# A convolution block in three stages: one instruction order across the seams, and what is loaded, stored and copied there

## The chip, the core and the metric

The kernel runs on one core of a Trainium2 chip. Its engines work side by side, each in its own order: TensorE (PE, matmuls; its weight loads are listed as PEld), VectorE (DVE), ScalarE (ACT), GpSimd (POOL) and SyncE (SP). SP and POOL start most transfers, and a transfer that must wait blocks what stands behind it on the engine that starts it. The metric is the device time of the whole program in microseconds, the median of several runs. A profile is one more execution, recorded by the hardware; its span runs from the first to the last instruction.

## The reference

The input x is 16 images of 192 channels and 64 by 64 pixels, float32. Cut to what matters:

```python
h = ln_over_channels(x)                                  # ln1
projected, gate = split(conv1x1(h, in_proj))             # 192 -> 384 channels
projected = depthwise3x3(projected, dw_k)
scanned = mix of four first-order recurrences of projected: along rows and columns, both ways
local = depthwise3x3(projected, le_k)
mixed = (scanned + local) * sigmoid(gate)
bn = (mixed - mean) / sqrt(var + 1e-5)                   # per channel, over all images and pixels
x = x + conv1x1(gelu(bn * bn_w + bn_b), out_proj)
h2 = ln_over_channels(x)                                 # ln2
x = x + conv1x1(gelu(conv1x1(h2, fc1)), fc2)             # 192 -> 768 -> 192
pooled = x.mean(over pixels)
w = a 3x3 kernel per image and channel, from a small net on pooled, four of its nine taps not zero
out = depthwise3x3(x, w) + bias
```

The batch norm needs the mean and the variance of a channel over all images, so nothing of the second half can start before the first half is done. This makes the seam between stages B and C.

## The kernel before

All is float32. Work falls into three stages, called A, B and C here.

**Stage A, projection.** 64 steps (`n` in the loop at L530), each eight image rows of two images, 512 pixels of each. `load_a` (L437) brings x, half on SP and half on POOL, three steps ahead. `turn` transposes pixels on PE for the variance, `project` (L471) multiplies by the input weights, and DVE and ACT evict the result into a staging buffer, scaled by the pixel's deviation (L485, L486). Four steps fill one block of 6.3 MB; 16 blocks alternate between two staging buffers, `stg0` and `stg1`. While a block is being filled, the one before is stored to HBM in four parts, one per step (`store`, L501): a part is a range of the 24 channel groups (`PARTS`, L47), and each part is a tensor of its own in HBM, `pg_d[0]` to `pg_d[3]`. Group 0 doesn't go to HBM: `store_first` (L495) copies it on chip into `low`. The first write of a block into its staging buffer waits for the stores of the block before last. After the last step its block is stored at once (L547 to L550). Beside the steps, small pieces of work (`beside`, from L394) prepare constants, among them `dv_d` and `lv_d`, from which stage B loads its banded matrices `dm` (depthwise) and `lm` (local and vertical), and load the weights of stage C (`load_weights`).

**Stage B, scans.** 96 steps (`k`, L711), each a pair of channels for all images; four pairs make a group. A step has `depthwise` of pair k+2 on PE, `tables` on ACT and two `scans` on DVE for pair k+1, `local` of pair k on PE, and for pair k-1 `vertical` on PE and `gate` on DVE, which multiplies with the sigmoid, writes the mixed rows over the group's own tile and takes the statistics (L666, L667). Three tiles hold groups in turn: part of `low`, `pg_o0` and `pg_o1`. `load_pg` (L567), on SP, loads group g+2 when group g-1 has been stored to `mixed_d` in HBM (L672, on POOL). Each group is 4 MB, each store 2 MB. `batch_norm` (L676) turns the statistics into a scale and a bias per channel, for the first 128 channels in the middle of the stage (L732) and for the other 64 at its end (L739): two matmuls, three DVE operations, more matmuls, the square root on ACT, and small DVE operations.

**Stage C, MLP and output.** Chunks of 512 pixels of an image pair. The mixed rows come back from `mixed_d` (`load_y`), DVE transposes them (`unmix`, L803, three 32 by 32 block transposes), ACT does batch norm and Gelu (L808, L809), `out_proj` multiplies (L819, L823) and DVE evicts into an image tile `ximg` (L826); `center`, `squares`, `normalize` are the second layer norm, `first` is fc1 (L884) with its Gelu (L887), `second` is fc2 (L774). The loop at L984 holds several chunks at different depths in one pass. Loads for the first chunks start at the end of stage B: `load_y` for `t` 0 and 1 at L735, and for `t` 2, which holds the last 64 channels, at L738, after the last group's store. The `ys` of chunks 2 to 7 lie in the second image tile until that is needed.

Each stage's instructions stand in a region of `manual_schedule` (L507, L704, L983), in which each engine keeps the written order. Buffers of a stage are released at its end, and a tile that takes their place waits for their last readers and writers. The transfers of a queue use eight semaphores in turn, so the ninth waits for the first.

Of the kernel before, what the change touches and what calls it, by code (L numbers as in the profile page):

```python
# [46 lines left out]
PARTS = ((1, 6), (6, 12), (12, 18), (18, NCG))  # L47
# [8 lines left out]
def conv_block_kernel(ctx: ExitStack, tc: tile.TileContext, x, prm, w_in, w_out, w_fc1, b_fc1, w_fc2, w1, bn1, w2, out):  # L56
# [7 lines left out]
    ORDER = {mybir.EngineType.PE, mybir.EngineType.DVE, mybir.EngineType.Activation, mybir.EngineType.SP,  # L64
             mybir.EngineType.Pool}

# [34 lines left out]
    wf2 = k2.tile([128, NFC, C], F32, tag="wf2", name="wf2")  # L101
# [71 lines left out]
    mats[0]["lm"] = lm_even  # L173
    bn_sc = cp.tile([128, 2], F32, tag="bn_sc", name="bn_sc")
# [9 lines left out]
    def load_lm(g):  # L184
        n = GC // 2
        for i, q in enumerate(HALF):
            v = lv_d[g, i, :, 0:1, :]
            src = bass.AP(v.tensor, v.offset, [[n, HW], [128 * n, 5], [1, HW * n]])
            (nc.sync, nc.gpsimd)[i].dma_start(mats[g % 2]["lm"][q].rearrange("p k m c -> p k (m c)"), src)
# [8 lines left out]
    def load_y(n, y, queues, ts=(0, 1, 2)):  # L198
# [4 lines left out]
        for t, q, i, c0 in ((0, slice(0, 128), 0, 0), (1, slice(0, 128), 1, 0), (2, HALF[0], 0, 128), (2, HALF[1], 1, 128)):  # L203
            if t in ts:
# [3 lines left out]
                for wh in range(2):  # L208
                    vw = v[32 * wh:32 * wh + 32].rearrange("w (q e) -> q w e", q=nq)
                    qd, k = (q, wh) if t < 2 else (HALF[wh], i)  # L210
                    if len(queues) == 1:
                        queues[0].dma_start(y[qd, t, k], vw)
                    else:
                        for b in range(nq):
                            p0 = qd.start + 32 * b
                            queues[b % 2].dma_start(y[p0:p0 + 32, t, k], vw[b])


    with ExitStack() as stage:
# [5 lines left out]
        w0 = wf2.rearrange("p m c -> p (m c)").rearrange("p (t n) -> p t n", t=3)  # L225
# [190 lines left out]
        for k in range(5):  # L416
            beside(40 + k, load_weights, k)
        beside(46, load_dm, 0)
        beside(47, load_lm, 0)
        beside(48, load_dm, 1)  # L420
        beside(50, lambda: finish_weights(0, bank()))
# [5 lines left out]
        stg = [stage.enter_context(tc.tile_pool(name=f"stg{i}", bufs=1)) for i in range(2)]  # L427
# [43 lines left out]
        def project(n):  # L471
            blk, part = divmod(n, per)
            if part == 0:
                both_i = stg[blk % 2].tile([128, 2, 2 * C, BR], F32, tag="stg", name="stg")
                stag[blk] = [both_i[:, i] for i in range(2)]
# [30 lines left out]

        with tc.manual_schedule(engines=ORDER):  # L507

            for dst, src in ((pt3, prm), (w0, w_in)):
                v = src.rearrange("(t p) n -> p t n", p=64)  # L510
                nc.sync.dma_start(dst[HALF[0]], v)
                nc.scalar.dma_start(dst[HALF[1]], v)
            make_identity(nc, ident)
            nc.vector.memset(mean_w, 1.0 / C)
            nc.vector.memset(ones, 1.0)
            nc.vector.memset(eps6, 1e-6)
            nc.vector.memset(eps5, 1e-5)
            nc.vector.memset(mask, 1.0)
            for k, r in ((0, 0), (1, HW - 1)):
                nc.vector.memset(mask[:, k, :, r:r + 1], 0.0)  # L520
            for c in range(3):
                load_a(c)
            centre = projection_weights()
            turn(0)
            for g in range(AR):
                variance(0, g)
            centre()
            deviation(0)

            for n in range(n_ac):  # L530
                if n + 3 < n_ac:
                    load_a(n + 3)
                blk, part = divmod(n, per)
                if blk:
                    if part == 0:
                        store_first(blk - 1)
                    store(blk - 1, part, (nc.gpsimd, nc.sync))
                    if part == per - 1:
                        stag.pop(blk - 1)
                if n + 1 < n_ac:  # L540
                    turn(n + 1)
                project(n)
                if n + 1 < n_ac:
                    deviation(n + 1)
                for f, args in side.pop(n, ()):
                    f(*args)
            store_first(blk)  # L547
            store(blk, 0, (nc.gpsimd, nc.sync))
            for d in range(1, len(PARTS)):
                store(blk, d, (nc.gpsimd, nc.gpsimd))  # L550


    with ExitStack() as stage:
        pg_odd = []
        kb = stage.enter_context(tc.tile_pool(name="kb", bufs=1))
        pg_odd.append(kb.tile([128, n_blk, 2, GC, BR], F32, tag="pg_o0", name="pg_o0"))
        wb = stage.enter_context(tc.tile_pool(name="wb", bufs=2))
        kc = stage.enter_context(tc.tile_pool(name="kc", bufs=1))
        late = {}
# [7 lines left out]
        def load_pg(g):  # L567
            s = grp[g]
            if g == 2:
                pg_odd.append(kc.tile([128, n_blk, 2, GC, BR], F32, tag="pg_o1", name="pg_o1"))  # L570
            s["pg"] = pg_even if g % 3 == 0 else pg_odd[g % 3 - 1]
            if g:
                d = [lo_ <= g < hi_ for lo_, hi_ in PARTS].index(True)
                lo_ = (g - PARTS[d][0]) * GE
                nc.sync.dma_start(s["pg"].rearrange("p n k c j -> p n (k c j)"),
                                  pg_d[d][:, :, :, lo_:lo_ + GE].rearrange("i b p e -> p (i b) e"))
# [51 lines left out]
        def lmul(k, m, src, dst, start, stop):  # L628
            g, c = divmod(k, hp_)
            for i, q in enumerate(HALF):  # L630
                for ih, o in enumerate(HALF):
                    nc.tensor.matmul(dst(bst[k]["ps"][i][o]), mats[g % 2]["lm"][q, m, :, c], src(q, ih), start=start, stop=stop)  # L632
# [25 lines left out]
        def gate(k):  # L658
# [10 lines left out]
            if c == hp_ - 1:  # L669

                for i0, i1 in ((0, n_half),) if g < NCG - 1 else ((0, 2), (2, n_half)):
                    nc.gpsimd.dma_start(mixed_d[i0:i1, :, :, g].rearrange("i b p e -> p (i b) e"),  # L672
                                        s["pg"][:, i0 * NB:i1 * NB, 0].rearrange("p n c j -> p n (c j)"))
                s.clear()

        def batch_norm(cls):  # L676

            chs = (slice(0, 128), slice(128, C))[cls]
            n = chs.stop - chs.start

            means = stats.rearrange("p c (e k) -> p k e c", k=3)[:, 1, :, chs]
            sums2 = stats.rearrange("p c (e k) -> p k e c", k=3)[:, 2, :, chs]
            dv = late["dev"][:, :, chs]
# [6 lines left out]
            nc.vector.scalar_tensor_tensor(dv, sums2, 2.0 / (n_half * HW), dv, ALU.mult, ALU.add)  # L690
            pq = psb.tile([128, CH], F32, tag="l", name="pq", bufs=4)
# [11 lines left out]

        with tc.manual_schedule(engines=ORDER):  # L704
            load_pg(0)
            load_pg(1)
            load_pg(2)
            mats[1]["lm"] = kc.tile([128, 5, HW, hp_], F32, tag="lm1", name="lm1")
            load_lm(1)
            late["dev"] = kc.tile([128, 2, C], F32, tag="dev", name="dev")  # L710
            for k in range(-2, n_bp + 1):  # L711
                if 0 <= k + 1 < n_bp:
                    tables(k + 1)
                if k >= 1:
                    vertical(k - 1)
                    gate(k - 1)
                    g, c = divmod(k, hp_)
                    if c == 0 and 0 < g < NCG - 1:
                        load_lm(g + 1)
                    if c == 0 and g + 2 < NCG:  # L720
                        load_pg(g + 2)
                    if c == hp_ - 2 and g + 2 < NCG:
                        load_dm(g + 2)
                if 0 <= k + 1 < n_bp:
                    scans(k + 1)
                if k + 2 < n_bp:
                    depthwise(k + 2)
                if 0 <= k < n_bp:
                    local(k)
                    sigmoid(k)  # L730
                if k == n_bp - 5 * hp_:
                    batch_norm(0)  # L732
                if k == n_bp - hp_:

                    load_y(0, y_low, (nc.sync,), (0, 1))  # L735
                    load_x2(0)
                    load_x2(1)
            load_y(0, y_low, (nc.sync, nc.gpsimd), (2,))  # L738
            batch_norm(1)  # L739
# [53 lines left out]
    def unmix(n):  # L793

        c, y = n % NCH, ys[n // 2]
        mx = mxs[n % 2]
        r0 = (c % 2) * CR
        for t in range(3):

            kinds = ("p k (c j) -> p j k c", "p (r k w) -> p r k w") if t < 2 else ("p k (c j) -> p k j c", "p (k r w) -> p k r w")  # L800
            blocks = y[:, t].rearrange(kinds[0], j=BR)
            blocks = blocks[:, r0:r0 + CR] if t < 2 else blocks[:, :, r0:r0 + CR]
            nc.vector.transpose(mx[:, t].rearrange(kinds[1], k=2, w=32), blocks)  # L803
        st[n].update(mx=mx)
# [168 lines left out]
    def at(f, n, *a):  # L973
        if 0 <= n < n_ch:
# [7 lines left out]

    with tc.manual_schedule(engines=ORDER):  # L983
        for n in range(-3, n_ch + 1):  # L984
            ended = (n - 1) // NCH if n >= NCH and (n - 1) % NCH == NCH - 1 else None
            if n + 5 < NCH and (n + 5) % 2 == 0:
                load_y(n + 5, ys[(n + 5) // 2], (nc.sync, nc.gpsimd) if n == -3 else (nc.gpsimd,))
# [84 lines left out]
```

## Time and profile before

| | |
|---|---|
| median of 3 runs | 3854.52 us (3853.04 to 3855.56) |
| the profiled execution | 3864.51 us, span 3862.7 us |
| stage A, 30 to 640 us | PE busy 595.2 of 610 us, DVE 457.0, ACT 239.8, DMA 241 GB/s |
| stage B, 720 to 1330 us | PE busy 602.8 of 610 us, DVE 600.3, ACT 514.1, DMA 272 GB/s |
| stage C, 1450 to 3800 us | PE busy 2349.8 of 2350 us, DVE 1442.5, ACT 906.1, DMA 58 GB/s |
| end of A, start of B, 640 to 720 us | PE busy 63.5 of 80 us, mean clock 0.89 |
| end of B, start of C, 1330 to 1450 us | PE busy 93.1 of 120 us, mean clock 0.87 |

A line of the timeline has the start and the length of a run of instructions, the engine, the source line, the operation, output and inputs, and in brackets how long the engine had been idle before and what ended that. `SPq` and `POOL ... DMA` lines are the starting of transfers, not the transfers. A line of the waits has the total, the number and the longest. A line of the windows has the stretch, then for PE, PEld, DVE, ACT and POOL the busy time and number of instructions, then PE's granted clock (1.00 is full), the mean busy share of the 16 DMA engines and the GB/s moved.

### The profile page before, as it was taken

What the parts mean: (1) busy time and instruction counts of PE and PEld (TensorE: products, weight loads), DVE (VectorE), ACT (ScalarE), POOL (GpSimd) and SP (SyncE); (2) the same over time, 40 slices, a digit from 0 to 9 for tenths busy, and PEclk for the clock granted to TensorE, in tenths of its full rate; (3) what the DMA queues carried; (4) which work ended last, traced back from release to release, by engine and by line L of the source; (5) the groups of instructions that cost most, each with busy time, mean ns of one, the idle gap of its engine ahead of it and who ended that gap; (6) DMA issues with size and microseconds to landing.
All of it is one profiled execution on the core that took longest, in us unless ns stands there. A gap on an engine that the chain in (4) does not pass through costs nothing.

```text
span 3862.7 us, 61441 instructions
## 1 busy us (share of the span) xinstructions
PE 3768.0 (98%) x25484; PEld 1750.0 (45%) x25484; DVE 2675.2 (69%) x4140; ACT 1775.7 (46%) x1879; POOL 411.3 (11%) x665
## 2 busy tenths in 40 slices
PE   8999999899999979999999999999999999999998
PEld 5565666566655533333333333333333333333333
DVE  6776776899999955456656756665765765674754
ACT  3333334788887833334334434333343433343442
POOL 2333332111101020000000000000000000000000
PEclk9999999999999989999999999999999999999999
DMA  6789987999999840112212222222222221221212
GB/s 152 234 235 237 269 263 245 270 274 283 274 284 258 230 99 21 53 43 60 74 55 63 66 65 59 69 58 64 70 55 59 70 69 44 76 72 44 69 28 71
DMA packets 305542, 491.13 MB, mean 127 GB/s; under 512 B 45344, under 2 KB 200208, under 8 KB 305264
## 3 DMA queue, kind: packets, MB, share of 16 engines
q1 hardware_dynamic: 246640, 290.58, 28.4%
q0 software_dynamic: 58208, 196.28, 19.0%
q8 instruction: 202, 3.31, 0.4%
q14 instruction: 76, 0.62, 0.1%
q10 hardware_dynamic: 416, 0.33, 0.0%
HBM read 284.98 MB, written 197.92 MB: 125 GB/s over the span
## 4 chain that ended last, share of the span: by engine, by line
PE 94%; DMA 3%; DVE 2%; issue 1%; ACT 0%; SPq 0%; POOL 0%; DVEq 0%; POOLq 0%; ACTq 0%
PE ps_f L884 27%; PE ps_f L774 25%; PE ps_pj L480 12%; PE ps_l L632 10%; PE ps_d L588 6%; PE ps_o L823 5%; PE ps_o L819 3%; PE ps_xt L455 2%; PE ps_v L846 1%; PE ps_m L846 1%; DMA pg_o<-pg_d 1%; DMA xa<-in_x_dram 1%; DMA out_dram<-ol 0%; PE ps_k L774 0%; DMA pg_d<-stg 0%
## 5 line engine op out<-in xcount | busy, mean ns | idle before, releaser
L884 PE MATMUL ps_f<-h,wf 64*128 64x512 f32 x4608 | 1050.7, 601 | 4.3 <-DVE h L874 3.6
L774 PE MATMUL ps_f<-gl,wf 128*64 128x512 f32 x4608 | 1021.5, 592 | 0.0
L887 ACT ACTIVATE gl<-ps_f,bf 128x1024 f32<-128x1024 f32 x384 | 428.2, 1115 | 1175.0 <-PE ps_f L884 1174.2
L884 PEld LDWEIGHTS ps_f<-h,wf 64*128 64x128 f32 x4608 | 433.7, 187 | 564.1 <-issue 561.9
L826 DVE SCALAR_TENSOR_TENSOR ximg<-ps_o,pt,low 128x256 f32<-128x256 f32 x384 | 168.3, 480 | 629.2 <-PE ps_o L823 629.1
L774 PEld LDWEIGHTS ps_f<-gl,wf 128*64 128x64 f32 x4608 | 330.5, 137 | 580.0 <-issue 537.9
L480 PE MATMUL ps_pj<-wi,xa 64*128 64x384 f32 x3072 | 518.5, 490 | 10.6 <-DVE stg L485 10.4
L486 ACT ACTIVATE stg<-ps_pj,rsa 128x384 f32<-128x384 f32 x256 | 239.5, 940 | 382.9 <-PE ps_pj L480 347.9
L480 PEld LDWEIGHTS ps_pj<-wi,xa 64*128 64x128 f32 x3072 | 293.1, 188 | 208.2 <-DVE stg L485 16.4
L68 DVE SCALAR_TENSOR_TENSOR o<-ximg,taps,o 128x1024 f32<-128x1024 f32 x252 | 323.7, 1285 | 86.0 <-ACT o L944 78.5
L948 POOL DMA_DIRECT2D out_dram<-o x168 | 87.9, 528 | 2134.3 <-DVE o L68 2131.5
L485 DVE TENSOR_SCALAR stg<-ps_pj,rsa 128x384 f32<-128x384 f32 x256 | 228.6, 893 | 109.6 <-PE ps_pj L480 84.7
L873 DVE RECIPROCAL rs<-rs 128x512 f32<-128x512 f32 x64 | 214.3, 3348 | 64.9 <-ACT rs L872 64.9
L623 DVE TENSOR_TENSOR_SCAN v<-tab,q 128x1024 f32<-128x1024 f32 x96 | 218.2, 2273 | 10.8 <-ACT tab L611 10.8
L625 DVE TENSOR_TENSOR_SCAN v<-tab,q 128x1024 f32<-128x1024 f32 x96 | 217.5, 2265 | 0.0
L823 PE MATMUL ps_o<-low,wo 128*64 128x256 f32 x1536 | 209.6, 394 | 0.0
L611 ACT ACTIVATE tab<-mask,dec_b 128x1024 f32<-128x1024 f32 x192 | 209.3, 1141 | 0.0
L588 PE MATMUL ps_d<-pg_o,dm 64*64 64x384 f32 (+2 forms) x2560 | 181.5, 424 | 13.1 <-DMA pg_o<-pg_d 13.1
L462 DVE BATCH_NORM_STATS2 st<-ps_xt 128x6 f32<-128x192 f32 x512 | 173.5, 339 | 23.8 <-PE ps_xt L455 23.8
L855 DVE TENSOR_TENSOR h<-ximg,ps_m 128x768 f32<-128x768 f32 x128 | 116.1, 948 | 98.7 <-PE ps_m L846 98.7
L588 PEld LDWEIGHTS ps_d<-pg_o,dm 64*64 64x64 f32 x2560 | 132.7, 198 | 91.3 <-issue 67.7
L803 DVE STREAM_TRANSPOSE low<-low 128x512 f32<-128x512 f32 x174 | 167.5, 1015 | 1.8
(182 smaller groups left out, 3771.7 us busy)
## 6 DMA issues: line engine op xcount, KB each, us to landing
pg_o<-pg_d SPq DMA_DIRECT2D x16, 4096.0 KB
low<-in_x_dram SPq DMA_DIRECT2D x128, 384.0 KB
out_dram<-o POOLq DMA_DIRECT2D x168, 256.0 KB, 3.7
pg_d<-stg POOLq DMA_DIRECT2D x102, 384.0 KB, 7.6
pg_d<-stg SPq DMA_DIRECT2D x90, 384.0 KB
mixed_d<-pg_o POOLq DMA_DIRECT2D x15, 2048.0 KB, 11.8
low<-mixed_d SPq DMA_DIRECT2D x116, 256.0 KB
low<-pg_d SPq DMA_DIRECT2D x7, 4096.0 KB
```

What stands on the lines that cost most here:

```text
L68: nc.vector.scalar_tensor_tensor(o, in0, scalar, in1, ALU.mult, ALU.add, **kw)
L480: nc.tensor.matmul(ps[i], pixels(n, t, g)[q], wi[q, t].rearrange("p g k c -> p (g k c)"), start=(t == 0), stop=(t == 2))
L485: nc.vector.tensor_scalar_mul(stag[blk][0][:, :, j], ps[0], rs[:, g, 0:1])
L486: nc.scalar.activation(stag[blk][1][:, :, j], ps[1], AF.Copy, scale=rs[:, g, 1:2])
L588: nc.tensor.matmul(dst(ps[o, ih]), mats[g % 2]["dm"][q, di + 1, :, ch], src(s["pg"][q, :, 0, ch]), start=(di == 0), stop=stop)
L623: nc.vector.tensor_tensor_scan(vf, tab, q, 0.0, ALU.mult, ALU.add)
L625: nc.vector.tensor_tensor_scan(vf[:, ::-1], tab[:, ::-1], q[:, ::-1], 0.0, ALU.mult, ALU.add)
L632: nc.tensor.matmul(dst(bst[k]["ps"][i][o]), mats[g % 2]["lm"][q, m, :, c], src(q, ih), start=start, stop=stop)
L774: nc.tensor.matmul(ps[q], w(i), rhs(i), start=start, stop=stop)
L823: nc.tensor.matmul(ps[q, wh].rearrange("p (r w) -> p r w", w=32), wo[:, 64 * t:64 * t + 64], cols(rows(s["mx"][:, i]))[:, :, wh], start=Fa ...
L884: nc.tensor.matmul(pf[:, i], wf1[q, t, 128 * m:128 * m + 128], s["h"][q, t], start=(t == 0), stop=(t == 2))
L887: nc.scalar.activation(gl, pf, AF.Gelu, bias=bf1[:, m:m + 1])
```

## The change

1. One region of `manual_schedule` is entered before stage A and holds to the end, instead of three.
2. `PARTS` is (1,2), (2,9), (9,16), (16,21), (21,24): the first part is group 1 alone. In the first step of a block two parts are stored, and then 7, 5 and 3 groups. After the last step only group 0 and the part of group 1 are stored at once (POOL); the other 16 stores follow on SP behind the load of group 1.
3. That load is split: images 0 to 5 of each half on SP, 6 and 7, which the last blocks write, on POOL.
4. The odd blocks' staging buffer `mid` lasts to the end of B: it is then the third group tile, `lm` of the odd groups and `dev`. So group 2's load waits for the last block's stores out of it.
5. `wf2` and `lm` of group 1 share a tile `place`: `lm` of group 1 is loaded in step 49 of A, and `wf2` in B at group 3 instead of in step 42 of A.
6. `batch_norm` is split: `spread` (matmuls and three DVE operations) and, one step later, the rest.
7. At the end of B the rows that chunks 0 and 1 need of the last group are copied on chip from its tile into `y_low` by four transfers, ahead of its store to HBM, which is one transfer instead of two; the other rows of `t` 2 are loaded half a group earlier. The transposes of chunk 0 stand between the steps of the second batch norm.
8. In C, chunk 2's transposes and Gelu move from before `out_proj` of chunk 1 to the end of that pass, and the memset of `pool2` moves three passes later.

```diff
-PARTS = ((1, 6), (6, 12), (12, 18), (18, NCG))
+PARTS = ((1, 2), (2, 9), (9, 16), (16, 21), (21, NCG))
...
-    wf2 = k2.tile([128, NFC, C], F32, tag="wf2", name="wf2")
+    place = k2.tile([128, 5 * HW * (GC // 2)], F32, tag="place", name="place")
+    wf2 = place[:, 0:NFC * C].rearrange("p (m c) -> p m c", m=NFC)
...
+    SB_ = 2 * 2 * C * BR
+    mid = ce.tile([128, SB_], F32, tag="mid", name="mid")
+    mats[1]["lm"] = mid[:, NPG:NPG + 5 * HW * (GC // 2)].rearrange("p (k m c) -> p k m c", k=5, m=HW)
+    dev = mid[:, NPG + 5 * HW * (GC // 2):NPG + 5 * HW * (GC // 2) + 2 * C].rearrange("p (e c) -> p e c", e=2)
+    lm_first = place.rearrange("p (k m c) -> p k m c", k=5, m=HW)
+    lm_of = lambda g: lm_first if g == 1 else mats[g % 2]["lm"]
...
+    LASTC = 32 - GC
+    def load_y(n, y, queues, ts=(0, 1, 2), last=32):
...
+                    if last < 32:
+                        for b, ncb in ((0, 32), (1, last)):
+                            p0 = qd.start + 32 * b
+                            queues[0].dma_start(y[p0:p0 + 32, t, k, 0:ncb * BR], vw[b, :, 0:ncb * BR])
...
+    def turn_back(y, mx, half, t):
+        kinds = ("p k (c j) -> p j k c", "p (r k w) -> p r k w") if t < 2 else ("p k (c j) -> p k j c", "p (k r w) -> p k r w")
+        blocks = y[:, t].rearrange(kinds[0], j=BR)
+        r = slice(half * CR, (half + 1) * CR)
+        nc.vector.transpose(mx[:, t].rearrange(kinds[1], k=2, w=32), blocks[:, r] if t < 2 else blocks[:, :, r])
+    ctx.enter_context(tc.manual_schedule(engines={
+        mybir.EngineType.PE, mybir.EngineType.DVE, mybir.EngineType.Activation, mybir.EngineType.SP, mybir.EngineType.Pool}))
...
-        for k in range(5):
+        for k in (0, 1, 3, 4):
             beside(40 + k, load_weights, k)
...
+        beside(49, load_lm, 1)
...
-                both_i = stg[blk % 2].tile([128, 2, 2 * C, BR], F32, tag="stg", name="stg")
+                if blk % 2:
+                    both_i = mid.rearrange("p (i o j) -> p i o j", i=2, j=BR)
+                else:
+                    both_i = stg.tile([128, 2, 2 * C, BR], F32, tag="stg", name="stg")
...
                 if part == 0:
                     store_first(blk - 1)
-                store(blk - 1, part, (nc.gpsimd, nc.sync))
+                    store(blk - 1, 0, (nc.gpsimd, nc.sync))
+                store(blk - 1, part + 1, (nc.gpsimd, nc.sync))
...
         store_first(blk)
-        store(blk, 0, (nc.gpsimd, nc.sync))
-        for d in range(1, len(PARTS)):
-            store(blk, d, (nc.gpsimd, nc.gpsimd))
+        store(blk, 0, (nc.gpsimd, nc.gpsimd))
...
+        def load_pg(g, queue=nc.sync, i0=0, i1=n_half):
...
             if c == hp_ - 1:
-                for i0, i1 in ((0, n_half),) if g < NCG - 1 else ((0, 2), (2, n_half)):
-                    nc.gpsimd.dma_start(mixed_d[i0:i1, :, :, g].rearrange("i b p e -> p (i b) e"),
-                                        s["pg"][:, i0 * NB:i1 * NB, 0].rearrange("p n c j -> p n (c j)"))
+                if g == NCG - 1:
+                    for i in range(2):
+                        for wh in range(2):
+                            w0_ = 32 * wh
+                            (nc.sync, nc.gpsimd)[wh].dma_start(y_low[2 * w0_ + 32:2 * w0_ + 64, 2, i, LASTC * BR:],
+                                                              s["pg"][w0_:w0_ + 32, i * NB, 0].rearrange("p c j -> p (c j)"))
+                nc.gpsimd.dma_start(mixed_d[:, :, :, g].rearrange("i b p e -> p (i b) e"),
+                                    s["pg"][:, :, 0].rearrange("p n c j -> p n (c j)"))
...
         load_pg(0)
-        load_pg(1)
+        load_pg(1, nc.sync, 0, n_half - 2)
+        load_pg(1, nc.gpsimd, n_half - 2, n_half)
+        for d in range(1, len(PARTS)):
+            store(blk, d, (nc.sync, nc.sync))
         load_pg(2)
-        mats[1]["lm"] = kc.tile([128, 5, HW, hp_], F32, tag="lm1", name="lm1")
-        load_lm(1)
...
+                if c == 0 and g == 3:
+                    load_weights(2)
...
             if k == n_bp - 5 * hp_:
-                batch_norm(0)
+                spread(0)
+            if k == n_bp - 5 * hp_ + 1:
+                batch_norm(0)
...
+            if k == n_bp - hp_ // 2:
+                load_y(0, y_low, (nc.sync,), (2,), LASTC)
-        load_y(0, y_low, (nc.sync, nc.gpsimd), (2,))
-        batch_norm(1)
+        turn_back(y_low, mxs[0], 0, 0)
+        spread(1)
+        turn_back(y_low, mxs[0], 0, 1)
+        batch_norm(1)
+        turn_back(y_low, mxs[0], 0, 2)
...
         if n == -3:
             border(ximg[0])
+        if n == 0:
             nc.vector.memset(pool2, 0.0)
...
+        early_, late_ = (n + 3, None) if n != -1 else (None, 2)
         at(load, n + 3)
-        at(unmix, n + 3)
+        at(unmix, early_)
...
-        at(bn_gelu, n + 3)
+        at(bn_gelu, early_)
...
         at(out_proj, n + 2, 2)
         at(second, n, 1)
+        at(unmix, late_)
+        at(bn_gelu, late_)
```

## The prediction

> **What bounds the kernel now.** I read the busy shares first, then the waits of TensorE (PE) longest first, then the order of time at each place where PE waits.
>
> ```profile
> PE 3768.0 (98%) x25484; PEld 1750.0 (45%) x25484; DVE 2675.2 (69%) x4140; ACT 1775.7 (46%) x1879; POOL 411.3 (11%) x665
> ```
>
> PE is busy 3768 of 3862.7 us, so a change that leaves its matmuls alone has at most 95 us of idle time to win, plus matmuls that ran at a lower clock. The longest entries of PE's waits:
>
> ```profile
> PE ps_d L588 <- DMA pg_o<-pg_d: 13.1, 1, 13.1
> PE ps_o L819 <- ACT low L809: 10.7, 1, 10.7
> PE ps_pj L480 <- DVE stg L485: 10.4, 6, 3.4
> ...
> PE pq L695 <- DVE dev L690: 6.3, 2, 5.6
> ```
>
> These are the seam from projection (A) to scans (B), the seam from B to the MLP (C), block starts inside A, and the first batch norm. The 2350 us of C from 1450 to 3800 hold 2349.8 us of PE work: nothing is to be had there. In order of time, the first seam:
>
> ```profile
> 663.53 21.01 SPq L575 DMA_DIRECT2D pg_o<-pg_d  x2
> ...
> 693.11 4.70 PE L588 MATMUL ps_d<-pg_o,dm 64*64 64x512 f32 x40 [13.13 <-DMA pg_o<-pg_d]
> ...
> 702.19 0.69 DVE L666 TENSOR_TENSOR low<-ps_l,sg 128x512 f32<-128x512 f32 x1 [13.06 <-PE ps_l L632]
> ```
>
> SP's load of group 1 leaves at 663.5, when the last block's stores into that part have landed, and the group arrives at 693. PE stood from 680.0, VectorE (DVE) from 689.1. DVE is what counts in B: its gates follow each other every 7.0 us, while PE's pair of 2.61 (depthwise) and 4.28 (local and vertical) in the chain is 6.89.
>
> **First seam.** After the change the part in front of group 1 holds one group. Behind the last projection come the first stores (4 of 64 KB), four 64 KB stores of group 1 on POOL, and the load (six of eight images on SP, two on POOL); the other 16 stores stand behind the load on SP. Up to group 1 that is 0.26 + 0.26 + 4.19 = 4.72 MB. The windows from 655 on moved 177 GB/s in the first 5 us and from 665 to 705 on average 337; three of them:
>
> ```profile
> 680.00:685.00 5.00, 0.00 (x0) 0.00 (x0) 4.93 (x6) 3.76 (x4) 1.37 (x2) 0.83 1.11 357
> 685.00:690.00 5.00, 0.00 (x0) 0.00 (x0) 4.12 (x2) 0.00 (x0) 0.00 (x0) 0.50 1.05 248
> 690.00:695.00 5.00, 1.89 (x12) 0.78 (x16) 0.00 (x0) 0.00 (x0) 0.00 (x0) 0.50 1.10 348
> ```
>
> (The last three columns are PE's clock, DMA share and GB/s.) So group 1 lands at 655 + 5 + 3.83/0.337 = 671, some 2 us later for the first stores sharing the engines; PE asks at 680. The rule that speaks against it is in the Trainium skill, DMA: Bandwidth & Descriptors, "Issuing engines are not separate DMA queues": transfers started from SP and POOL run on the same 16 engines and interleave. If the stores took an equal share from the start, 0.5 + 2 x 4.19 MB would have to pass, the group would land at 655 + 5 + 8.0/0.337 = 684, PE would lose 4 us and DVE, which has 1.9 us in hand there (PE could finish the products that the next gate reads at 687.2, DVE is free at 689.1), 2 us. I take the earlier value, since the stores are on SP's own queue behind the load. Worth: DVE's 13.1 us. The clock adds nothing: the 40 matmuls after the gap took 4.70 us where 2.61 is usual, but that lies within DVE's 13.06.
>
> What is late next is group 2. Its load goes to the lasting buffer and waits on SP for nearly all 16 stores from it; behind it on SP stand dm, lm and group 3. Before its issue 4.72 + 5.77 = 10.5 MB pass: 660 + 9.6/0.337 = 688.5, 2 us to complete, then 4.19/0.337 + 2 = 14.4: it lands at 705, dm with it at about 706. DVE, unstalled, reaches the gate whose products stand behind group 2's first depthwise in PE's order at 689.1 + 4 x 7.0 = 717.1, and PE needs 2.6 + 2.7 + 1.9 = 7.2 us before that: the limit is 709.9. Spare 4 us, so 0 loss; with 248 GB/s throughout, 9.7 lost.
>
> **lm of group 1, wf2.** lm's two loads (640 KB) move from the seam to step 49 of A, wf2's 576 KB from A into B on SP at group 3, in front of group 5's load. Each group's load has some 14 us in hand (issued four steps of 7 ahead). Nothing; if that spare were gone, 2 us once.
>
> **Batch norm in two steps.**
>
> ```profile
> 1221.97 1.02 PE L695 MATMUL pq<-ones,dev 128*128 128x1 f32 x4 [5.64 <-DVE dev L690]
> ...
> 1226.43 0.69 DVE L666 TENSOR_TENSOR pg_o<-ps_l,sg 128x512 f32<-128x512 f32 x1 [2.15 <-PE ps_l L632]
> ```
>
> The gates before and after stand at 1213.24 and 1226.43: 13.2 instead of 7.0, cost 6.2. Split, DVE still does 0.58 + 0.42 + 0.60 and gaps = 1.7 in the first step, PE finds dev done one step on; there DVE waits about 1 us for the Sqrt (table load 1.28 behind the sigmoids) and does 0.8 of small operations: 3.5. Gain 2.7; bounds 1.2 (the DVE wait is 2.5) and 4.2.
>
> **Second seam.** T is the end of the last statistics, 1357.8.
>
> ```profile
> 1357.40 2.31 POOL L672 DMA_DIRECT2D mixed_d<-pg_o  x2 [21.76 <-DVE pg_o L666]
> ...
> 1367.94 0.06 DVE L990 MEMSET pool<- 128x6 f32 x1 [5.32 <-DMA low<-mixed_d]
> ...
> 1372.02 1.13 PE L819 MATMUL ps_o<-low,wo 64*64 64x256 f32 x8 [10.70 <-ACT low L809]
> ...
> 1397.39 8.45 PE L884 MATMUL ps_f<-h,wf 64*128 64x512 f32 x24 [3.64 <-DVE h L874]
> ```
>
> Now: rows out to HBM and back, DVE's memset waits for them, three transposes (0.94 each), Gelu, output projection at T+14.2, first fc1 matmul at T+39.6. After: the last rows go on chip, four 16 KB copies (two on SP, two on POOL). No such copy is in the trace; the nearest, the 64 KB first stores on chip, took 2.6 us on SP, and the 64 KB loads 4.0 on POOL: between T+2 and T+4.6. They are covered: DVE does a transpose (to T+1.0), the spread (to 2.4), a second transpose (3.4), the norm's ends (4.8), and only then the third (5.8). Gelu follows the table load at 5.3 and 6.6, so output projection starts at T+7.3 and could be evicted at 10.4.
>
> A new wait stands there: the buffer of the last group now lies under the image tile, so the first eviction on DVE must wait until the store of that group to HBM has been read out. It is one piece now and issued after two copies, at T+0.7. It took 10.5 us here as two pieces, 11.8 as the usual one, 14.1 once: it ends at T+11.2 to 14.8, and everything on DVE is queued behind it. I take T+12, as nothing else is loading. From the first eviction to fc1 the trace has 1375.10 to 1397.39, 22.3; of this 2.9 go, because the transposes of chunk 2 move behind the normalisation, and 1.2, because PE has the second product ready: 18.2. Put behind, the transposes fit DVE's 5.2 us gap at 1402 to 1407.5, and their Gelu fits ACT's 9.6 us gap. PE then starts fc1 at about T+30.6, 9.0 earlier; bounds 6 and 10.5. The 8.45 us for 24 matmuls (5.35 warm) I leave: the Trainium skill, TensorE: Matmul & The Clock Gate, Part 1, has the array fall to half clock after some 3.4 us of idleness, and the wait of 7 us stays longer. If instead the shorter wait kept it warm, it would be 3 us more.
>
> **Stores in falling parts.** Five block starts make PE wait 1.5 to 3.4 us, 10.2 in sum, with 1.7 at a lower clock.
>
> ```profile
> 323.00:361.00 38.00, 34.62 (x211) 21.11 (x211) 24.63 (x74) 13.26 (x18) 13.03 (x21) 0.96 0.98 254
> 361.00:400.00 39.00, 36.87 (x239) 22.95 (x237) 27.30 (x83) 14.35 (x20) 15.02 (x24) 1.00 0.98 227
> ```
>
> In the blocks of these five the DMA share is 0.95 to 1.08 at 224 to 289 GB/s. A step of 9.4 us now brings 2.36 MB, afterwards 3.15, 2.62, 2.10 and 1.57. At 2.6 MB per step the last store lands at 1.57 + 0.07 over 2.6, 5.9 us into its step instead of 8.5. At 2.1 per step (224 GB/s) the backlog at the end is 1.04 MB in either case and nothing is won. Only the last of the five, at 289, has room, and the one at 254 a little. I take 3; bounds -4 (64 more stores, of 1 KB rows) and 11.
>
> One ordered region by itself moves nothing on PE: the engines' order in A and most of B is the same.
>
> **Sum.** 13.1 + 2.7 + 9.0 + 3.0 = 27.8 us. The profiled execution took 3864.5 (span 3862.7 and 1.8 around it) and becomes 3836.7; it is 10 us above the median of the runs, so for the median 3854.5 - 27.8 = 3827.
>
> **Rivals.** (1) Group 2 takes the place of group 1: at 248 GB/s it is 9.7 us late, 3836. For it: one window at that rate, a load that waits for everything. Against: six of the eight from 665 on are at 348 to 390. (2) DMA is the limit anyway: A gives nothing and the last store takes 14.1, so the second seam gives 6: 13.1 + 2.7 + 6 = 21.8, 3833. For it: shares of 1.0 in A. (3) The shorter stores clear A of waits and the clock stays up: 11 + 3 instead of 3: 3816. (4) Slower than before: group 2's load, waiting on SP for all of the stores, lands more than 27.8 us past 709.9, after 738: 13.8 MB at under 185 GB/s. No window from 660 to 705 is that slow: the lowest are 248 and 288. (5) The change doesn't do what it says: the six-image load still waits for the last block's stores. They are four of 64 KB and land by 661; the group would come at 676, still in time.
>
> **Numbers.** Forecast 0.68, (1) 0.11, (2) 0.12, (3) 0.05, (4) 0.02, and 0.02 for a no-change sum of lesser misses. Range: lowest 13.1 + 4.2 + 10.5 + 11 + 3 gives 3813; highest 9.7 lost with A at nothing and the seam at 6: 12.1 gained, 3842. 3813 to 3841 leaves out less than 2 in 10. Within 0.2% (7.7 us, about what runs of this kernel can tell from no change) 0.02, slower 0.02, faster 0.96.
>
> **What would show it.** No wait of PE on group 1; its load issued near 657 and landed by 673; depthwise of group 2 without a wait; gates at the first norm 10.5 apart; a store to HBM ending the wait of the first output eviction; fc1 some 31 us after the last statistics; waits at block starts in A still near 7 us. It is wrong if the load of group 1 leaves after 665, if group 2 lands after 710, or if A changes by more than 10.

## The result, and the profile after

The changed kernel takes 3831.6 us (median of 4 runs, 3827.9 to 3832.6); the kernel before took 3855.0 beside it (4 runs, 3853.0 to 3856.5). The ratio is 0.9938, with a 95% interval of 0.9921 to 0.9955: 23.5 us less. Predicted were 3827, in a range of 3813 to 3841. The profiled execution of the changed kernel took 3827.9 (span 3826.1), 36.6 less span than the one of before.

TensorE's busy time and its longest waits, of the page and of the waits of PE:

```profile
PE 3764.0 (98%) x25484; PEld 1762.9 (46%) x25484; DVE 2676.8 (70%) x4140; ACT 1780.3 (47%) x1879; POOL 420.2 (11%) x683
```

```profile
PE pb L278 <- DVE wi L275: 8.9, 1, 8.9
PE ps_f L920 <- DVE h L910: 4.6, 1, 4.6
PE pb L397 <- DVE wf L361: 4.3, 3, 1.4
PE pm L717 <- DVE stats L691: 4.2, 1, 4.2
PE ps_o L855 <- ACT low L845: 3.8, 1, 3.8
...
PE ps_pj L509 <- DVE stg L514: 3.4, 3, 1.7
```

The first of these waits is in the preparation of A and was there before (8.7). The wait of 13.1 us on group 1 is gone, that of the output projection fell from 10.7 to 3.8, and that on the first norm's `dev` from 5.6 to under 1. Block starts in A show 3.4 instead of 10.4; the experiments show that this last one must not be read as the others are.

The first seam in order of time: SP, then POOL, then PE's weight loads, which carry the start of each matmul.

```profile
646.06 1.12 SPq L527 DMA_DIRECT2D low<-mid  x2
647.53 0.43 SPq L599 DMA_DIRECT2D pg_o<-pg_d  x1
648.01 27.77 SPq L533 DMA_DIRECT2D pg_d<-mid  x16
677.52 0.39 SPq L599 DMA_DIRECT2D mid<-pg_d  x1
...
655.79 0.92 POOL L599 DMA_DIRECT2D pg_o<-pg_d  x1 [6.33 <-DMA pg_d<-mid]
...
669.66 0.35 PEld L612 LDWEIGHTS ps_d<-pg_o,dm 64*64 64x64 f32 x6
```

A's last projection ended at 645.1, against 654.5 before. SP's six images of group 1 left 2.5 us later. POOL's two images left 10.7 us after A's end, because POOL's own stores had to land first, and took 13.7 us to land: 669.4, just ahead of the first matmul that reads the group. DVE's gates run through at 7.0 us.

The first norm, on DVE:

```profile
1190.58 0.66 DVE L690 TENSOR_TENSOR low<-ps_l,sg 128x512 f32<-128x512 f32 x1
...
1199.20 0.68 DVE L690 TENSOR_TENSOR pg_o<-ps_l,sg 128x512 f32<-128x512 f32 x1
...
1206.71 0.16 DVE L733 RECIPROCAL bn_sc<-bn_sc 128x1 f32<-128x1 f32 x1 [0.36 <-ACT bn_sc L732]
...
1207.37 0.69 DVE L690 TENSOR_TENSOR pg_o<-ps_l,sg 128x512 f32<-128x512 f32 x1
...
1214.39 0.67 DVE L690 TENSOR_TENSOR pg_o<-ps_l,sg 128x512 f32<-128x512 f32 x1
```

From the gate before to the third behind it are 23.8 us, where before had 27.2 (1213.24 to 1240.46).

The second seam; T, the end of the last statistics, is 1331.8:

```profile
1332.44 1.75 POOL L701 DMA_DIRECT2D mixed_d<-mid  x1
...
1336.87 3.82 DVE L237 STREAM_TRANSPOSE low<-low 128x512 f32<-128x512 f32 x4 [0.31 <-issue]
1343.25 1.66 DVE L862 SCALAR_TENSOR_TENSOR ximg<-ps_o,pt,low 128x256 f32<-128x256 f32 x4 [2.56 <-issue]
...
1339.10 1.13 PE L855 MATMUL ps_o<-low,wo 64*64 64x256 f32 x8 [3.84 <-ACT low L845]
...
1361.31 7.87 PE L920 MATMUL ps_f<-h,wf 64*128 64x512 f32 x24 [4.61 <-DVE h L910]
```

Output projection starts at T+7.3 (T+14.2 before), the first eviction at T+11.5 (T+17.3), fc1 at T+29.6 (T+39.6). DVE's 2.56 us in front of the eviction has no named releaser, but the store into `mixed_d` took 10.7 us and landed at 1343.16, 0.1 before it. The end follows T by 2494.3 us; before it was 2504.9.

### The profile page after: what moved, and what is told of

The parts are those of the page before. It is cut to its first block, busy times and chain, and to the rows that moved or that the text cites. A ratio compares the mean times of both kernels' runs of the same rounds, so it can differ in the third digit from the quotient of the medians.

```text
span 3826.1 us, 61482 instructions
## 1 busy us (share of the span) xinstructions
PE 3764.0 (98%) x25484; PEld 1762.9 (46%) x25484; DVE 2676.8 (70%) x4140; ACT 1780.3 (47%) x1879; POOL 420.2 (11%) x683
## 4 chain that ended last, share of the span: by engine, by line
PE 95%; DMA 2%; DVE 2%; issue 0%; ACT 0%; POOL 0%; SPq 0%; POOLq 0%; DVEq 0%; ACTq 0%
PE ps_f L920 27%; PE ps_f L817 26%; PE ps_pj L509 12%; PE ps_l L656 10%; PE ps_d L612 6%; PE ps_o L859 5%; PE ps_o L855 3%; PE ps_xt L481 2%; PE ps_v L882 1%; PE ps_m L882 1%; DMA xa<-in_x_dram 0%; PE ps_k L817 0%; DVE ol L65 0%; DVE v L647 0%; DMA ximg<-mixed_d 0%
## 5 line engine op out<-in xcount | busy, mean ns | idle before, releaser
L817 PE MATMUL ps_f<-gl,place 128*64 128x512 f32 x4608 | 1021.5, 592 | 0.0
L817 PEld LDWEIGHTS ps_f<-gl,place 128*64 128x64 f32 x4608 | 330.5, 137 | 580.0 <-issue 537.9
L647 DVE TENSOR_TENSOR_SCAN v<-tab,q 128x1024 f32<-128x1024 f32 x96 | 218.3, 2274 | 10.7 <-ACT tab L635 10.7
L515 ACT ACTIVATE stg<-ps_pj,rsa 128x384 f32<-128x384 f32 x128 | 120.2, 943 | 189.6 <-PE ps_pj L509 176.6
L515 ACT ACTIVATE mid<-ps_pj,rsa 128x384 f32<-128x384 f32 x128 | 120.9, 944 | 182.5 <-PE ps_pj L509 172.2
L469 POOL DMA_DIRECT2D xa<-in_x_dram x192 | 119.8, 630 | 369.1 <-PE ps_pj L509 308.3
L941 DVE SCALAR_TENSOR_TENSOR ximg<-ps_f,pt,ximg 128x512 f32<-128x512 f32 x192 | 134.1, 748 | 36.2 <-PE ps_f L817 35.8
```

Of the source, the lines that this page charges most:

```text
L515: nc.scalar.activation(stag[blk][1][:, :, j], ps[1], AF.Copy, scale=rs[:, g, 1:2])
L647: nc.vector.tensor_tensor_scan(vf, tab, q, 0.0, ALU.mult, ALU.add)
L817: nc.tensor.matmul(ps[q], w(i), rhs(i), start=start, stop=stop)
```

## Experiments

Two readings of each profile carry them: A's end (the end of the last projection matmul on PE), and the rest (the time of the profiled execution less A's end). The last column is the rest less that of the changed kernel.

| kernel | A's end | rest | rest less 3182.8 |
|---|---|---|---|
| before | 654.5, 651.1 | 3210.0, 3213.0 | 27.2, 30.2 |
| changed | 645.1, 653.9, 657.2 | 3182.8, 3182.7, 3182.8 | 0 |
| even parts | 662.2 | 3183.3 | 0.5 |
| falling parts alone in the kernel before | 662.9 | 3212.0 | 29.2 |
| load of group 1 behind the stores | 648.1 | 3194.7 | 11.9 |
| norm in one step | 649.0 | 3189.1 | 6.3 |
| chunk 2 early | 647.4 | 3191.0 | 8.2 |
| rows by HBM | 646.4 | 3189.0 | 6.2 |
| few stores | 640.3 | 3182.7 | 0 |
| last store first | 654.5 | 3186.9 | 4.1 |
| the same with filler matmuls | 645.9 | 3186.2 | 3.4 |

The rest is the same to 0.1 us in three executions of the changed kernel, and what the change gained lies in it: 13.1 at the first seam, 3.4 at the first norm and 10.6 at the second seam make 27.1 of the 27.2 between the two first profiles. A's end is not the same: it moves by 12 us in one kernel. The kernel before took medians of 3855, 3867, 3856 and 3863 us in four sets of runs, so only times of one set, or rests, are compared. (The rows from even parts to falling parts shared a set with the second of the changed kernel, those from the load of group 1 to rows by HBM had one of their own, and those from few stores on shared one with the third.)

### Is A shorter, and do the falling parts make it so?

The kernel before, once more:

> The kernel before, unchanged, for a second profile of it. The first profiled execution of it (span 3862.7) was 10 us above the median of its runs; of the 36.6 us between the two profiled spans, 9.4 lie in stage A (first depthwise after the gap at 658.99 against 649.52), while the medians differ by 23.5. Theory S (the ten us are chance, and sit in A's block starts): span near 3853, depthwise at 649 to 652, waits at block starts well under 10. Theory D (A was 9 us slower before because of its parts): depthwise at 657 to 660 again, and the ten us are found in the MLP stage.

One profiled time, 3864.1; A ended at 651.1, with waits of 9.0 at block starts. Neither theory is right as written: the time was no lower, yet A ended 3.4 earlier, and the lost part was found at the first norm (the gate step behind the 13.4 took 8.2, not 7.0) and in front of fc1 (T+41.8, not T+39.6). The changed kernel, once more:

> The changed kernel, unchanged, for a second profile of it and five rounds. Both theories: 3831 +- 2, ratio 0.994. Stage A: S has its end vary by several us between executions of one kernel (depthwise after the gap anywhere in 648 to 656); D has it at 649 to 650 again.

3838.2 (5 runs), ratio 0.9927 (0.9912 to 0.9941); A's end 653.9. That is theory S: A's end differs between executions of one kernel. In another set it was 657.2. Even parts:

```diff
-PARTS = ((1, 2), (2, 9), (9, 16), (16, 21), (21, NCG))
+PARTS = ((1, 2), (2, 6), (6, 12), (12, 18), (18, NCG))
```

> The changed kernel with A's stores in even parts again: of groups 1 to 23, 5, 6, 6 and 6 groups per step as before, instead of 8, 7, 5 and 3. My forecast (falling parts give 3 us): 3834.5. Theory D (they give the 9.4 us by which A is shorter in the profiles): 3841, block-start waits 10 again. Theory S (they give nothing, A differed by chance): 3831 +- 2.

3840.0 beside the changed kernel's 3838.2; ratios to before 0.9933 (0.9919 to 0.9948) and 0.9927 (0.9912 to 0.9941): no difference that these runs can tell. The profile's 662.2 is one draw. The falling parts alone, in the kernel before:

```diff
-PARTS = ((1, 6), (6, 12), (12, 18), (18, NCG))
+PARTS = ((1, 2), (2, 9), (9, 16), (16, 21), (21, NCG))
...
-                    store(blk - 1, part, (nc.gpsimd, nc.sync))
+                        store(blk - 1, 0, (nc.gpsimd, nc.sync))
+                    store(blk - 1, part + 1, (nc.gpsimd, nc.sync))
```

> The kernel before with the falling parts alone (2 to 8, 9 to 15, 16 to 20, 21 to 23, group 1 for itself); all else as before, so the seams keep their waits, except that the load of group 1 has only its own part's stores to wait for. Forecast: A gives 3, and the first seam up to 8 more if the load may leave once its own part is stored. Theory D: 9 from A. Theory S: nothing from A. So 3852 (forecast without the seam), 3846 (D), 3855 (S), and up to 8 less in each if the load of group 1 leaves before the other stores have landed.

3871.2 (21 runs), ratio 1.0011 (1.0004 to 1.0017): 4.4 us above before's 3866.7 of the same set, where every case had it faster or the same. The first seam became longer:

```profile
665.08 5.24 POOL L504 DMA_DIRECT2D pg_d<-stg  x10
...
668.35 24.76 SPq L576 DMA_DIRECT2D pg_o<-pg_d  x2
...
703.67 5.07 PE L589 MATMUL ps_d<-pg_o,dm 64*64 64x512 f32 x40 [15.72 <-DMA pg_o<-pg_d]
```

The load left 5.5 us after A's end instead of 9.0, yet group 1 was read 40.8 us after it instead of 38.6, and the gate's step was 23.1 where before had 20.15. In both kernels SP's load runs beside the block's other stores, which POOL hands out. This is how the two queues shared the DMA engines from 674 to 684 (q0 is POOL's queue, q1 is SP's; packets, MB, share of the 16 engines):

```profile
q0 software_dynamic: 646, 3.21, 82.9%
q1 hardware_dynamic: 667, 0.68, 19.2%
```

Both moved nearly the same number of packets (131 in all are under 512 B), but those of the stores are rows of 5 to 7 KB and those of the load are rows of 1 KB, so the load got little over a sixth of the bytes. The kernel before shows the same from 670 to 676: 393 and 400 packets, 1.93 and 0.41 MB.

The seam alone does not explain the 4.4 us, though: the rest of this profile, 3212.0, lies between the two of the kernel before. By these rests A took 2.4 to 5.4 us more. So the falling parts gave A nothing, and together with the fifth part they seem to have cost something; which of the two did it was not separated. What holds A, then?

```diff
+            if d >= 2 and blk + 1 < n_ac // per:
+                return
...
-                lo_ = (g - PARTS[d][0]) * GE
+                if d >= 2:
+                    d, lo_ = 1, (g - 9) % 7 * GE
+                else:
+                    lo_ = (g - PARTS[d][0]) * GE
```

> The changed kernel with less for A's DMA to do: the stores of groups 9 to 23 are left out in all blocks but the last (groups 9 to 23 are then read from the part of groups 2 to 8, so their values are those of other channels). Theory L (A is held by the transfers, whatever their split into parts, and so by what the chip's DMA gives in that run): no waits at block starts but those at the very start, A's end at about 643 to 645 in every run, and the time at the lowest that the changed kernel has shown, 3826 to 3829. Rival (the waits at block starts are of the hand-over on DVE and ACT itself, not of the stores): A's end still anywhere in 645 to 654, waits of 3 to 7.

3823.2 (4 runs within 2.5 us), ratio 0.9899 (0.9887 to 0.9912). A ended at 640.3 and waited 0.3 us at block starts. Theory L, and both forecast numbers were too cautious by 3. Windows of A, few stores (the last two columns are DMA share and GB/s), and then of the changed kernel:

```profile
300.00:400.00 100.00, 100.00 (x644) 62.55 (x644) 76.44 (x227) 41.02 (x55) 35.24 (x55) 1.00 0.75 161
400.00:500.00 100.00, 100.00 (x642) 62.37 (x640) 75.78 (x223) 40.84 (x54) 32.70 (x56) 1.00 0.74 187
```

```profile
300.00:400.00 100.00, 98.69 (x632) 62.38 (x632) 74.54 (x224) 39.17 (x54) 44.95 (x72) 1.00 1.01 255
400.00:500.00 100.00, 98.26 (x624) 61.37 (x620) 74.36 (x220) 39.89 (x52) 37.96 (x66) 1.00 0.99 274
```

With the DMA engines three quarters busy, PE hardly stands and runs agree; with them full, A of the changed kernel loses 5 to 17 us, by what the transfers happen to give. Falling parts removed none of that, in either kernel. A's waits of 10.4 in one profile and 3.4 in the other were chance; three profiles of the changed kernel have 3.4, 7.1 and 11.6.

### The first seam: small part, or place in the queue?

```diff
-        load_pg(1, nc.sync, 0, n_half - 2)
-        load_pg(1, nc.gpsimd, n_half - 2, n_half)
         for d in range(1, len(PARTS)):
             store(blk, d, (nc.sync, nc.sync))
+        load_pg(1, nc.sync, 0, n_half - 2)
+        load_pg(1, nc.gpsimd, n_half - 2, n_half)
```

> The changed kernel with the load of group 1 put behind the other 16 stores of the last block on SP; its part still holds one group. Theory Q (the place in the queue makes the gain): SP takes 27.8 us to hand out the 16 stores, so the load leaves some 30 us after A's end, PE waits 17 to 22 us on group 1 and DVE loses 15 to 20. Theory P (the small part makes the gain: the load waits for four 64 KB stores only): nothing lost, no wait. Theory E (the 16 engines are shared, whatever the order): the load lands about 38 us after A's end, PE loses about 13.

3843.8 against 3856.0 of before, ratio 0.9969 (0.9957 to 0.9981), half of the gain.

```profile
650.23 22.91 SPq L533 DMA_DIRECT2D pg_d<-mid  x16
673.54 0.40 SPq L599 DMA_DIRECT2D pg_o<-pg_d  x1
...
686.74 4.34 PE L612 MATMUL ps_d<-pg_o,dm 64*64 64x512 f32 x40 [13.30 <-DMA pg_o<-pg_d]
```

P is out. The load left 25.4 us after A's end and was read at 38.6; the gate's step was 20.0, which is before's loss of 13 us back in full. Q is the mechanism, with its sizes too large (SP handed the stores out in 22.9 us). E named the size, but not the reason: with the same bytes and the load ahead on SP, the group is there after 24.4. So four arrivals of group 1 after A's end are measured: 24.4 with the load ahead of the stores on one queue, 38.6 behind them, and 38.6 (the kernel before) and 40.8 (falling parts) beside stores from another queue. PE asks at about 25.

The trace's packets show what the 24.4 is made of. In the ten profiles with the load ahead, all 3072 packets of 1 KB of SP's six images had moved 14.4 to 15.3 us after A's end. POOL's two images left only at 10.6 to 11.3, then moved beside SP's stores, and landed at 22.7 to 25.8; PE's first read came at 24.2 to 26.0. So POOL's quarter sets the arrival, and it comes in time by tenths. Whether all eight images on SP would come earlier was not tried.

### The norm

```diff
             if k == n_bp - 5 * hp_:
                 spread(0)
-            if k == n_bp - 5 * hp_ + 1:
                 batch_norm(0)
```

> The changed kernel with the first batch norm in one step again. From the profiles: the step between gates is 13.2 again and the next 7.0, where the changed kernel has 8.6 and 8.2, so 3.4 us more (forecast 2.7). Rival: the gain is not of the split, and the steps stay as they are (0).

3836.3, ratio 0.9947 (0.9932 to 0.9962). The steps are 13.4 and 8.1, as in the second profile of before, against 8.6 and 8.2: 4.7 us; another 1.3 of the rest is in the second seam, whose lines the edit does not touch.

### The second seam, one part at a time

```diff
-        early_, late_ = (n + 3, None) if n != -1 else (None, 2)
+        early_, late_ = n + 3, None
```

> The changed kernel with the transposes and the Gelu of chunk 2 ahead of the output projection's sums again. Forecast: the three transposes (2.9 us) stand in DVE's chain from the first output eviction to fc1, which grows from 18.1 to 21.0, fc1 at T+32.4, and 2.9 us more to the end. Rival: they only fill gaps in DVE (waits of 0.4 and 1.5 stand in that chain): 1 us or less.

3838.6, ratio 0.9952 (0.9937 to 0.9967); fc1 at T+38.3, rest 8.2 longer. Both readings fall:

```profile
1351.14 1.04 DVE L237 STREAM_TRANSPOSE low<-ximg 128x512 f32<-128x512 f32 x1 [0.19 <-issue]
1353.39 1.04 DVE L237 STREAM_TRANSPOSE low<-ximg 128x512 f32<-128x512 f32 x1 [1.21 <-DMA ximg<-mixed_d]
1356.99 1.03 DVE L237 STREAM_TRANSPOSE low<-ximg 128x512 f32<-128x512 f32 x1 [2.56 <-DMA ximg<-mixed_d]
```

The transposes don't only take their 2.9 us: they wait for chunk 2's rows, which come from HBM and are fetched when the last store has landed (it landed at 1345.88, SP's first fetch left at 1346.13). In the kernel before, where the output projection came later, they found their rows there and ran without a wait:

```profile
1381.10 2.88 DVE L803 STREAM_TRANSPOSE low<-ximg 128x512 f32<-128x512 f32 x3
```

In this run the next eviction of the output projection stands behind them, and PE waits 7.3 for it. The other part, undone alone (the last store in two pieces, the last rows fetched from HBM behind it):

```diff
-                            (nc.sync, nc.gpsimd)[wh].dma_start(y_low[2 * w0_ + 32:2 * w0_ + 64, 2, i, LASTC * BR:],
-                                                              s["pg"][w0_:w0_ + 32, i * NB, 0].rearrange("p c j -> p (c j)"))
...
-            if k == n_bp - hp_ // 2:
-                load_y(0, y_low, (nc.sync,), (2,), LASTC)
+        load_y(0, y_low, (nc.sync, nc.gpsimd), (2,))
```

> The changed kernel with the last group's rows fetched from HBM after the last store again (in two pieces), not copied on chip. Forecast: third transpose at T+12.5, output projection at T+14.2, first eviction at T+17.3 as before, fc1 18.1 behind that at T+35.4: 5.9 us more than the changed kernel. Rival: the store to HBM holds the first eviction in either case (T+11.5), and what is lost is only 2 us or less. Each of these two changes of the second seam alone; together they should give the 8.8 of the 10.0 us by which fc1 stands nearer to T.

3835.9, ratio 0.9946 (0.9929 to 0.9963). First eviction T+15.8, fc1 T+34.8: 5.3 later, near the forecast of 5.9. So, against the first profile of before, either part alone would have brought fc1 forward by 1.3 (T+39.6 to T+38.3) or by 4.7 (to T+34.8), and both bring 10.0: the fetch from HBM stands in the way twice, and is out of it only when both are done.

Is it the store that ends the wait before the first eviction? In the eight profiles in which it follows the copies, it landed at T+11.4 and the eviction started at T+11.5, which fits but is no test. The store put first:

```diff
                 if g == NCG - 1:
+                    nc.gpsimd.dma_start(mixed_d[:, :, :, g].rearrange("i b p e -> p (i b) e"),
+                                        s["pg"][:, :, 0].rearrange("p n c j -> p n (c j)"))
...
-                            (nc.sync, nc.gpsimd)[wh].dma_start(y_low
+                            nc.sync.dma_start(y_low
```

> The changed kernel with the last store to HBM put ahead of the four on-chip copies on POOL, all four copies on SP. If the store alone ends DVE's wait of 2.6 us before the first output eviction (it was issued at T+0.7 behind two copies), it now ends at T+10.4 at the earliest that PE allows, and fc1 starts 1.1 earlier, at T+28.5. Rival (the wait is of something else that lands at T+11.5, or the copies on SP come late for the third transpose): fc1 at T+29.5 or later.

3839.9 beside 3837.4, ratios 0.9945 (0.9933 to 0.9957) and 0.9937 (0.9923 to 0.9950); fc1 at T+33.5. The rival: the copies came late.

```profile
1340.64 4.21 SPq L700 DMA_DIRECT2D low<-mid  x4
...
1350.74 3.81 DVE L237 STREAM_TRANSPOSE low<-low 128x512 f32<-128x512 f32 x4 [4.60 <-DMA low<-mid]
```

Four copies of 16 KB kept DVE waiting until T+9.4, beside a 2 MB store that started before the last of them; in the changed kernel the copies on POOL, ahead of the store, landed in 1.7 and 3.2 us. Queue and order were changed at once here, so which of the two it is stays open, and so does what the eviction would gain from an earlier store. Filler matmuls in PE's gaps, on top of that kernel:

```diff
+            if cls == 1:
+                for _ in range(6):
+                    nc.tensor.matmul(pm_last[0][:, 256:512], ones, wf1[:, 0, 0:256], start=True, stop=True)
...
             pf = ps2.tile([128, 2, CH], F32, tag="f1", name="ps_f1", bufs=2)
+            for _ in range(9 if n == 0 and m == 0 else 0):
+                nc.tensor.matmul(pf[:, 0, 0:256], wf1[:, 0, 0:128], wf1[:, 0, 0:256], start=True, stop=True)
```

> The same with matmuls of no use in PE's two gaps of the second seam: 6 of 128x256 behind the norm's last sums (gap of 3.8 to 4.4 us), 9 in front of the first fc1 matmul (gap of 4.6). If the gaps let PE's clock fall, output projection's first pair takes 1.7 instead of 3.1 and the 24 matmuls of fc1 5.4 instead of 7.9: the end some 2.5 us earlier than the kernel of the same call without them (the first pair is hidden if the store still ends the eviction's wait). If not, they change nothing or cost up to 2.

```profile
1363.44 4.15 PE L927 MATMUL ps_f<-wf 128*128 128x256 f32 x18
1367.52 5.42 PE L930 MATMUL ps_f<-h,wf 64*128 64x512 f32 x24
```

The 9 fillers are recorded as 18 pieces. fc1's 24 matmuls took 5.42 instead of 7.82 in the kernel without fillers. The windows of these 24, without fillers and then with them (PE's clock is the third number from the end):

```profile
1374.80:1382.60 7.80, 7.79 (x24) 3.37 (x24) 7.66 (x12) 3.74 (x4) 2.68 (x4) 0.69 0.94 153
1367.50:1373.00 5.50, 5.44 (x25) 2.24 (x24) 5.41 (x9) 1.73 (x2) 2.62 (x4) 1.00 1.05 157
```

As they began 0.5 later, relative to T, and the end came 1.5 earlier (T+2496.8, T+2498.3). Output projection's first pair took 0.66 and 1.61 instead of 1.13 and 1.97. Its time, 3838.1, doesn't differ from the others of the set, in which A's part scatters more. The last of the set, the changed kernel:

> The changed kernel once more, as the measure for the three others on the same chip: ratio 0.993 to 0.994, A's end in 645 to 655, the second seam at T+11.5 and T+29.6, end at T+2494.3.

3837.4 (6 runs, 3828.6 to 3847.1), ratio 0.9937; the second seam exactly as forecast, A's end at 657.2, above. No kernel here is shown to beat the changed one with all of its work done. The fillers without the moved store were not tried.

## Why the prediction came out as it did

The mechanism and the sum for what lies behind A are right: forecast 13.1 + 2.7 + 9.0 = 24.8, measured 27.2 between the two first profiles. The median moved by 23.5 only; since the rest fell by at least 27.2, A took 3.7 or more of it back in those runs. In the later sets the same working leaves A between 1.4 gained and 5 lost. That the total came within 4.3 us of the forecast 27.8 is in part luck: it had 2.4 too little behind A and 6.7 too much in A.

- **First seam, 13.1.** Right in size: the step of 20.15 became 7.0, and the loss returned as 13.0 when the load was put behind the stores. The estimate inside it was right for SP's part alone: I had group 1 land 16.5 us after A's end, 18.5 with the first stores sharing, and SP's six images had moved by 15.1. The group landed at 24.4, against a need of about 25. What I left out is that POOL's quarter of the load waits until POOL's own stores land, leaves 10.7 after A's end and then moves beside SP's stores. The spare of 9 us that I saw there doesn't exist; that nothing was lost is luck by tenths.
- **The rule weighed there** (the Trainium skill, DMA: Bandwidth & Descriptors, "Issuing engines are not separate DMA queues") holds between queues: the load beside POOL's stores came at 38.6 and 40.8. The equal share that I set against it did not hold: the packets were about equal in number, and of the bytes the load got little over a sixth. My reason for setting its full price aside, that the stores stand behind the load on SP's own queue, holds too: 24.4 against 38.6.
- **Group 2, rival (1) and (4).** Its load left at 677.5 and it was first read at 697.3, with gates at 7.0 throughout. No loss. Rival (5) is out by the issue at 647.5 for SP's part, and true for POOL's, which did wait for stores.
- **Batch norm, 2.7.** 3.4 against the first profile of before, 4.7 when undone. The mis-sized term is DVE's wait for Sqrt: 1 us forecast, 0.36 measured. The gates are 8.6 and 8.2 apart, where I wrote 10.5, although my own sum has 1.7 in one step and 1.8 in the next.
- **Second seam, 9.0.** fc1 10.0 nearer to T, the end 10.6. Output projection came at T+7.3 as forecast, a wait that ends as the store lands held the eviction to T+11.5 where I took T+12, and from there to fc1 it took 18.1 (18.2 forecast; with T+12 that makes T+30.2, where I wrote T+30.6). The 2.9 for chunk 2's transposes is what they took in the kernel before, so it was right in this sum. As the price of leaving them in place it was wrong: with the earlier output projection they would have cost 8.7, since they then wait for HBM. The clock was left out of the sum rightly: the 24 matmuls still took 7.87 us (5.42 when warm, where I wrote 5.35), though PE's waits were 3.8 and 4.6 and not 7. That the gaps cost this is now measured, a granted clock of 0.69 against 1.00 with fillers; it agrees with the Trainium skill (TensorE: Matmul & The Clock Gate, Part 1), which has the array at half clock after an idle window of some 3.4 us.
- **Falling parts, 3.0.** This step failed: in place of 3 gained, by the rests A lost 3.7 or more in the runs of the result. I read waits of a single profile as a fixed cost of block starts and moved bytes between steps to remove them. They belong to a stage whose transfers are at the limit, and they differ from run to run. What the trace said against it (a DMA share of 1.0, and nothing won at 224 GB/s) I used only to make the term smaller. Rival (2) had this half right, and its other half, a late last store, wrong.

## What to carry to other kernels

Put a load that the next stage waits for ahead of the stores of the last one, on the same queue: here SP's part of it had moved by 15 us, and the same stores from another queue, or ahead of it, made the group 14 to 16 us later. Beside stores of another queue, look at the size of the packets: here the load with the smaller ones got the smaller share. When work is moved, ask first what it waits for where it stands; its duration may be the smaller part. And a stage with its DMA engines full gives another time in each run, so split the time at a fixed event (here A's end) before crediting an edit with a difference of two profiles.

## What was not expected of the hardware

A's end varied from 645.1 to 657.2 in one kernel while the other 3183 us repeated to 0.1. Sixteen stores held SP's queue for 22.9 to 27.8 us, where the issue of the load alone took 0.4. Two queues side by side moved equally many packets, not equally many bytes (646 and 667 packets, 3.21 and 0.68 MB). And copies of 16 KB, which landed in 1.7 and 3.2 us ahead of a 2 MB store, kept DVE waiting beside such a store until 1350.74, 5.9 us after the last of them was handed out.
